# Float32 adjacency products as three one-pass products of split operands: a four-layer graph network on one core

## The chip, the core and the metric

The kernel runs on one core of a Trainium2 chip. The metric is the device time of one execution in microseconds (us). "Clock" is the mean granted TensorE clock of a stretch, as a share of full speed. Two kernels are compared by runs that alternate on the same chip.

## The reference

2708 nodes with 512 float32 features pass four layers, each followed by a residual and a layer norm. `adj` is a sparse float32 matrix, held densely.

```python
# layer 0: hypergraph mean
head = mask / maximum(sqrt(sum(mask * mask, -1)), EPS)      # mask = adj > 0
inc  = adj + head
x = LN(x + (inc @ x) / sum(inc, -1))
# layer 1: attention over adj's pattern, and a GCN, each with a gate
ga, gb = sigmoid([adj @ x, x] @ Wa.T + ba), sigmoid([adj @ x, x] @ Wb.T + bb)
h = x @ W_sa;  s = (h @ a_left)[:, None] + (h @ a_right)[None, :]
e = where(adj != 0, exp(-leaky_relu(s, 0.01)), 0)
attn = e / (sum(e, 1) + 1e-5)
x = LN(x + sigmoid(ga * (attn @ h) + gb * (adj @ (x @ W_gcn) + b_gcn)))
# layer 2: x W0 + A(x W1 + A(x W2 + A(x W3))), written as three hops
# layer 3: ((A x + x) / deg + x) @ W + b, relu
```

There are seven sweeps over a 2708 x 2708 matrix: one in layer 0, two in layer 1, three hops, one in layer 3. With 22 row tiles of 128 rows (the last has 20), a sweep is 22 x 22 = 484 products of a 128x128 block with 128x512 features.

## The kernel before

The sweeps' operands are float32 (only the 0/1 masks that are counted are 2-byte). The transposed adjacency block is the stationary operand and the features, resident in SBUF, are the moving one:

```python
def sweep_mm(ps, lhs, rhs, m, q, first=True, last=True):
    ...
    for k in range(k0, k1):
        kr = rows[k]
        nc.tensor.matmul(ps[:w], lhs[q][:kr, k - k0, :w], rhs[k][:kr], start=first and k == 0,
                         stop=last and k == NT - 1)
```

Row sums (layer 0's degree and the attention's denominator) are mostly VectorE work. Each piece of 5 or 6 blocks is reduced to one block, and TensorE only finishes the sum over partitions, four small products per row tile:

```python
def part_sum(t, q, w):
    ...
    nc.vector.tensor_reduce(s[:, :w], t[:, :nk, :w].rearrange("p k i -> p i k"), AX.X, ALU.add)
    return s

def row_sum(parts, w, eps):
    ps = psum.tile([P, 1], F32, name="ps_s", bufs=2)
    for n, s in enumerate(parts):
        nc.tensor.matmul(ps[:w], s[:, :w], ones, start=n == 0, stop=n == len(parts) - 1)
    ...
```

Row m's masks, counts and edges are made while row m-1 or m-2 is multiplied. Layer 1 reads each adjacency row once and runs its two sweeps interleaved. A hop is nothing but `sweep_mm`, four transposes, four dense products and an eviction per row tile.

## Time and profile before

Median 3713.67 us, 3711.66 to 3713.99. The stages, from windows of the profile:

| stage | us | TensorE busy | VectorE busy |
|---|---|---|---|
| layer 0 | 592 | 97% | 64% |
| layer 1, both sweeps | 970 | 100% | 45% |
| x2 W3 | 90 | 96% | 20% |
| hops and layer 3 | 2058 | about 100% | 3% to 26% |

The lines behind it stand in the prediction. How to read them: a share near 100% with a chain of waits that is 99% TensorE means that, as things stand, nothing but less TensorE work can shorten the run.

### The profile page before, as it was taken

How to read it: one execution, taken by the hardware profiler on the slowest of the kernel's cores; microseconds unless marked ns; L12 is line 12 of the kernel's file. 1: busy time of each engine (PE TensorE's matmuls, PEld its weight loads, DVE VectorE, ACT ScalarE, POOL GpSimd, SP SyncE). 2: the span in 40 equal slices, each digit the busy share in tenths (PEclk: the TensorE clock that was granted, in tenths of full speed). 3: DMA queues.
4: the chain of work that ended last, by engine and by line, in shares of the span. 5: the costliest groups of instructions: out<-in, count | busy, mean ns of one | idle time of the engine just before them, and what ended most of it. 6: DMA issues, size and time to landing. Idle time of an engine off the chain costs nothing.

```text
span 3710.3 us, 25433 instructions
## 1 busy us (share of the span) xinstructions
PE 3679.8 (99%) x10340; PEld 1626.9 (44%) x10340; DVE 1057.5 (29%) x1807; ACT 265.2 (7%) x392; POOL 88.8 (2%) x249
## 2 busy tenths in 40 slices
PE   7999999999999999999999999999999999999999
PEld 3444444444444444344444434444344444344443
DVE  6676654444444444110000000000000001222222
ACT  0000001111111111110000000000000000000000
POOL 0000000000000000000000000000000000000000
PEclk9999999999999999999999999999999999999999
DMA  4222211111111110102222122222222221222220
GB/s 149 53 56 56 54 44 55 31 34 30 33 30 30 30 33 19 37 24 60 60 60 60 48 71 60 60 60 60 59 60 60 60 60 48 77 69 71 68 71 21
DMA packets 377865, 197.16 MB, mean 53 GB/s; under 512 B 27156, under 2 KB 368364, under 8 KB 377748
## 3 DMA queue, kind: packets, MB, share of 16 engines
q1 hardware_dynamic: 370278, 181.58, 18.8%
q10 hardware_dynamic: 7470, 13.95, 1.1%
q8 instruction: 82, 1.34, 0.1%
q14 instruction: 35, 0.29, 0.0%
HBM read 189.94 MB, written 5.55 MB: 53 GB/s over the span
## 4 chain that ended last, share of the span: by engine, by line
PE 99%; DMA 1%; DVE 0%; issue 0%; POOLq 0%; SPq 0%
PE acc L102 68%; PE ps_u L102 11%; PE acc L116 9%; PE ps_d L116 6%; PE ps_t L109 2%; PE ps_s L129 1%; PE ps_s L171 1%; PE ps_s L284 1%; PE ps_s L210 0%; DMA adj<-in_adjT 0%; DMA w<-in_w_hop 0%; PE ps_t L262 0%; PE ps_u L186 0%; DMA A<-in_x 0%; DVE tmp L192 0%; DVE y L380 0%
## 5 line engine op out<-in xcount | busy, mean ns | idle before, releaser
L102 PE MATMUL acc<-C,adj 128*128 128x512 f32 (+2 forms) x1936 | 855.4, 595 | 0.0
L102 PE MATMUL acc<-B,adj 128*128 128x512 f32 (+2 forms) x1936 | 853.5, 594 | 0.0
L102 PEld LDWEIGHTS acc<-B,adj 128*128 128x128 f32 (+2 forms) x1936 | 352.5, 186 | 462.3 <-issue 461.1
L102 PEld LDWEIGHTS acc<-C,adj 128*128 128x128 f32 (+2 forms) x1936 | 352.2, 186 | 462.7 <-issue 462.1
L102 PE MATMUL acc<-A,adj 128*128 128x512 f32 (+1 forms) x968 | 436.1, 600 | 2.3 <-DVE adj L194 2.3
L102 PE MATMUL acc<-C,edge 128*128 128x512 f32 (+1 forms) x968 | 436.0, 597 | 0.0
L102 PE MATMUL ps_u<-B,adj 128*128 128x512 f32 (+1 forms) x968 | 434.6, 595 | 0.0
L116 PE MATMUL acc<-w,xT 128*128 128x512 f32 (+1 forms) x704 | 324.7, 604 | 1.4 <-DMA w<-in_w_hop 1.4
L102 PEld LDWEIGHTS acc<-C,edge 128*128 128x128 f32 (+1 forms) x968 | 176.0, 185 | 248.0 <-issue 248.0
L111 ACT COPY xT<-ps_t 128x512 f32<-128x512 f32 (+1 forms) x154 | 87.7, 570 | 2748.9 <-PE ps_t L109 2741.6
L102 PEld LDWEIGHTS ps_u<-B,adj 128*128 128x128 f32 (+1 forms) x968 | 176.6, 186 | 229.3 <-issue 229.2
L102 PEld LDWEIGHTS acc<-A,adj 128*128 128x128 f32 (+1 forms) x968 | 174.2, 187 | 214.1 <-issue 195.6
L116 PE MATMUL ps_d<-w,xT 128*128 128x512 f32 (+1 forms) x528 | 243.5, 604 | 0.5 <-DVE y L380 0.5
L116 PEld LDWEIGHTS acc<-w,xT 128*128 128x128 f32 (+1 forms) x704 | 124.4, 186 | 182.6 <-issue 180.9
L358 DVE COPY C<-acc 128x512 f32<-128x512 f32 (+1 forms) x22 | 15.2, 692 | 494.2 <-PE acc L116 494.2
L358 DVE COPY B<-acc 128x512 f32<-128x512 f32 (+1 forms) x22 | 15.2, 691 | 494.2 <-PE acc L116 494.2
L116 PEld LDWEIGHTS ps_d<-w,xT 128*128 128x128 f32 (+1 forms) x528 | 92.8, 186 | 129.9 <-issue 128.4
L361 DVE TENSOR_TENSOR y<-acc,A 128x512 f32<-128x512 f32 (+1 forms) x22 | 15.2, 692 | 413.6 <-PE acc L116 413.4
L131 DVE TENSOR_SCALAR rd<-ps_s 128x1 f32<-128x1 f32 (+1 forms) x44 | 6.9, 157 | 431.2 <-PE ps_s L129 431.2
L122 DVE TENSOR_REDUCE part<-edge 128x128 f32<-128x768 f32 (+3 forms) x88 | 111.6, 1305 | 0.0
L122 DVE TENSOR_REDUCE part<-adj 128x128 f32<-128x768 f32 (+3 forms) x88 | 111.6, 1309 | 0.0
L372 DVE TENSOR_SCALAR edge<-adj 128x768 bf16<-128x768 f32 (+3 forms) x88 | 44.2, 509 | 208.4 <-PE ps_s L171 152.1
(72 smaller groups left out, 1477.5 us busy)
## 6 DMA issues: line engine op xcount, KB each, us to landing
adj<-in_adjT SPq DMA_DIRECT2D x252, 384.0 KB
adj<-in_adjT SPq DMA_DIRECT2D x126, 320.0 KB
adj<-in_adjT SPq DMA_DIRECT2D x126, 256.0 KB
A<-in_x ACTq DMA_DIRECT2D x21, 256.0 KB
out<-xa SPq DMA_DIRECT2D x21, 256.0 KB
w<-in_w_hop ACTq DMA_DIRECT2D x4, 1024.0 KB
adj<-in_adjT SPq DMA_DIRECT2D x126, 10.0 KB
w<-in_w_sa ACTq DMA_DIRECT2D x1, 1024.0 KB
```

Source lines behind the costliest of these rows:

```text
L102: nc.tensor.matmul(ps[:w], lhs[q][:kr, k - k0, :w], rhs[k][:kr], start=first and k == 0, stop=last and k == NT - 1)
L109: nc.tensor.transpose(ps[:, c, :w], src[:w, c * P : (c + 1) * P], ident[:w, :w])
L111: nc.scalar.copy(t[:, :, :w], ps[:, :, :w])
L116: nc.tensor.matmul(ps[:w], xT[:, c, :w], wt[:, c, :], start=first and c == 0, stop=c == DC - 1)
L122: nc.vector.tensor_reduce(s[:, :w], t[:, :nk, :w].rearrange("p k i -> p i k"), AX.X, ALU.add)
L129: nc.tensor.matmul(ps[:w], s[:, :w], ones, start=n == 0, stop=n == len(parts) - 1)
L131: nc.vector.tensor_scalar(rd[:w], ps[:w], eps, None, ALU.add)
L171: nc.tensor.matmul(ps[:w], mask[m][q][:, k - k0, :w], ones_bf, start=k == 0, stop=k == NT - 1)
L284: nc.tensor.matmul(pz[:w], xT[m][:, c, :w], wab_sb[:, c, :], start=c == 0, stop=c == DC - 1)
L358: nc.vector.tensor_copy(dst[m][:w], ps[:w])
L361: nc.vector.tensor_tensor(y[:w], ps[:w], x2[m][:w], ALU.add)
L372: nc.vector.tensor_scalar(t[:, : k1 - k0, :w], adj[m][q][:, : k1 - k0, :w], 0.0, None, ALU.not_equal)
```

## The change

A float32 product takes, as the prediction reads its 0.86 us, four passes of 0.215 us through the array. The intent is to take three: split each operand into a rounded high part and a remainder, take hi·H and lo·L into one PSUM bank and a mixed product mx·G into another, and recombine the two banks at eviction. The operands are float32r, a 4-byte type whose product takes one pass. Features are split once per sweep, adjacency blocks anew in every sweep, on VectorE.

```diff
+    def split(a, nk, h=None):
+
+        s = slot(F32, "s")
+        lo = slot(F32R, "lo")
+        mx = slot(F32R, "mx")
+        av = a[:, :nk, :].bitcast(F32)
+        nc.vector.tensor_scalar(s[:, :nk, :].bitcast(I32), a[:, :nk, :].bitcast(I32), HI, None, ALU.bitwise_and)
+        nc.vector.tensor_tensor(lo[:, :nk, :], av, s[:, :nk, :], ALU.subtract)
+        nc.vector.scalar_tensor_tensor(mx[:, :nk, :], s[:, :nk, :], C1, av, ALU.mult, ALU.subtract)
... (hi: a copy of s by ScalarE in layer 0, by DMA in attention, else the block itself)
     def sweep_mm(...)
-            nc.tensor.matmul(ps[:w], lhs[q][:kr, k - k0, :w], rhs[k][:kr], start=first and k == 0,
-                             stop=last and k == NT - 1)
...
+            nc.tensor.matmul(pq, hi[:kr, b, :], H[k][:kr], start=first, stop=False)
+            nc.tensor.matmul(pq, lo[:kr, b, :], L[k][:kr], start=False, stop=last)
+            nc.tensor.matmul(pv, mx[:kr, b, :], G[k][:kr], start=first, stop=last)
+            if rs is not None:
+                nc.tensor.matmul(rs, hi[:kr, b, :], ones_r[:kr], start=first, stop=False)
+                nc.tensor.matmul(rs, lo[:kr, b, :], ones_r[:kr], start=False, stop=last)
...
+    def evacuate(acc, w):
+
+        pq, pv = acc
+        t = row_tile("t")
+        nc.scalar.mul(t[:w], pv[:w], -SC)
+        y = row_tile("y")
+        nc.vector.scalar_tensor_tensor(y[:w], pq[:w], C1, t[:w], ALU.mult, ALU.add)
+        return y
...
+    def run(load, prepare, before=None, finish=None, wide=True, rowsum=False, moving=None, early=None, ahead=2):
...
+            loads(n + ahead + 3)
+            prep(n + ahead)
+            if q == 0:
+                acc[m] = accumulators(wide and m == 2)
+                rs[m] = bank("rs", [P, 2]) if rowsum else None
+            sweep_mm(acc[m], ops.pop((m, q)), q, rs[m])
...
+            step()
+            if q == NQ - 1:
+                steps += finish(m, acc.pop(m), rs.pop(m))
```

`prep` issues the splits two pieces ahead of the products, and `step` one part of the previous row's end. With it come, cut here: row sums by two-column TensorE products (`ones_r` is [P, 2]) in place of VectorE's reductions; three resident feature tensors H, L, G, so that the features themselves pass through DRAM; a blocked adjacency copy in DRAM, stored in layer 0 and read by the later sweeps; a ring of 16 slots shared by adjacency, splits and edges; layer 0's masks on ScalarE from a second load of the adjacency; two exponentials per block on ScalarE; attention aggregates x1 and multiplies by W_sa afterwards; plain sweeps start with three row tiles side by side.

## The prediction

> **What bounds the kernel now.** I read the busy shares first, then the 40 slices, the chain that ended last, the costliest groups, then windows cut at the seven stages and the timeline inside one sweep.
>
> The page's busy shares, two of its slice rows and the head of its chain:
>
> ```profile
> PE 3679.8 (99%) x10340; PEld 1626.9 (44%) x10340; DVE 1057.5 (29%) x1807; ACT 265.2 (7%) x392; POOL 88.8 (2%) x249
> ...
> PE   7999999999999999999999999999999999999999
> ...
> DVE  6676654444444444110000000000000001222222
> ...
> PE 99%; DMA 1%; DVE 0%; issue 0%; POOLq 0%; SPq 0%
> PE acc L102 68%; PE ps_u L102 11%; PE acc L116 9%; PE ps_d L116 6%; PE ps_t L109 2%; PE ps_s L129 1%; PE ps_s L171 1%; PE ps_s L284 1%; PE ps_s L210 0%; DMA adj<-in_adjT 0%; DMA w<-in_w_hop 0%; PE ps_t L262 0%; PE ps_u L186 0%; DMA A<-in_x 0%; DVE tmp L192 0%; DVE y L380 0%
> ```
>
> TensorE is full in every slice but the first. 79% of the chain is L102, the adjacency sweeps; 15% is L116, the dense products. VectorE is idle in the hops. So only less TensorE work can help, and VectorE has room to pay for it. The stages, as windows (layer 0, layer 1, x2 W3, three hops, layer 3; columns: length, then busy time of each engine, clock, DMA share, GB/s):
>
> ```profile
> 0.00:592.30 592.30, 572.74 (x2099) 272.63 (x2100) 379.82 (x643) 26.13 (x44) 29.65 (x75) 1.00 0.25 67
> 592.30:1562.00 969.70, 969.07 (x2580) 431.55 (x2578) 437.57 (x675) 176.46 (x238) 17.12 (x43) 1.00 0.12 32
> 1562.00:1652.10 90.10, 86.72 (x257) 41.09 (x258) 18.02 (x28) 12.46 (x22) 0.54 (x1) 0.98 0.03 12
> 1652.10:2161.50 509.40, 509.40 (x1234) 217.21 (x1233) 15.22 (x23) 12.54 (x22) 4.42 (x22) 1.00 0.23 60
> ...
> 3180.30:3710.30 530.00, 523.02 (x1716) 230.24 (x1714) 140.09 (x307) 12.54 (x22) 16.65 (x43) 1.00 0.23 63
> ```
>
> A hop is 100% TensorE. Inside it, the timeline shows the unit of work:
>
> ```profile
> 1666.12 0.19 PEld L102 LDWEIGHTS acc<-B,adj 128*128 128x128 f32 x1 [0.24 <-issue]
> 1666.55 0.19 PEld L102 LDWEIGHTS acc<-B,adj 128*128 128x128 f32 x1 [0.24 <-issue]
> 1666.98 0.19 PEld L102 LDWEIGHTS acc<-B,adj 128*128 128x128 f32 x1 [0.24 <-issue]
> ```
>
> One weight load and one 512-column matmul record every 0.43 us, the load hidden. A float32 product is two such records (484 products give x968 for a sweep in the page's groups), so 0.86 us. A row tile of a hop, 22 products, four transposes, four dense products, takes 509.4/22 = 23.15 us.
>
> **What the Trainium skill says.** "FP8 and Floating Point Precision", section TensorE Precision Notes: float32 takes four passes, while reduced-precision float32 reads the 4-byte value truncated to FP22. The trace fits four passes: 0.86 us is four times 0.215. "TensorE: Matmul & The Clock Gate", section Back-to-back issue gap: warm, N/2.4 + 2.5 ns, which is 216 ns at 512 columns; the trace agrees (0.43/2), at a granted clock of 0.999. (That section also gives 131 ns as a sustained figure; nothing here is near it.) "VectorE: DVE Perf Modes", the perf-mode tier table: float32 tensor_scalar in SBUF runs at twice the rate, tensor_tensor at the single rate. The trace agrees: over 768 elements 540 ns against 952.
>
> **The change, part by part.**
>
> (1) Sweep products. hi*H + lo*L into one bank, mx*G into another, recombined at eviction, gives the full product in three one-pass matmuls. 7 sweeps x 484 = 3388 products: removed 3388 x 0.862 = 2920 us; added 10164 x 0.217 (0.215 plus a little) = 2206 us. Gain 715 us, if a one-pass load hides too. The load row lasts 190 ns, but eight loads of the row sums' one-column products come in 0.97 us, so 0.12 us each is the rate; below 0.217, so I assume hidden. Per row tile 66 x 0.217 = 14.3 us against 19.0.
>
> (2) Row sums move to TensorE in layers 0 and 1: 2 x 484 x 2 = 1936 two-column products, each with its own weight load. Cost by that 0.12 us: 232 us, 5.3 us per row tile. They replace VectorE reductions (223 us) and 336 small records (40 us).
>
> (3) Dense products stay 616 float32 ones (layer 0 loses its W_sa product, the attention sweep gains it behind the aggregation): 3.54 us per row. Transposes go from 616 to 704: 0.44 us per four.
>
> (4) VectorE splits every adjacency block anew in every sweep: a bitwise tensor_scalar, a subtraction, a scalar_tensor_tensor. Durations from the 640 and 768 rows, scaled linearly: two-tensor operations 817 and 951 give 684 ns at 512 elements and 550 at 384; tensor_scalar 485 and 540 give 430 and 375. A piece of four blocks is 430 + 2 x 684 = 1.80 us, of three 1.48; a row tile, four and two of these, 10.1 us. Layer 0 and attention have two more two-tensor operations per piece: + 7.7. The hop with the degree mask: + 2.5. Each feature tile entering a sweep is split for 1.8 us, 39.5 us per sweep, six times. VectorE in all: 1562 + 339 + 54 + 237 + evictions 106 + norms 138 + some 190 = about 2630 us, 77% of the new time: busy, but beside TensorE.
>
> (5) DMA: layer 0 loads the adjacency twice and stores the blocked copy; attention adds 32 MB of SBUF-to-SBUF copies (484 blocks of 64 KB); features go through DRAM. Before, the windows moved 60 GB/s at a share of 0.23, so twice to three times that has room; in a plain sweep 1.4 MB per 18.3 us is 79 GB/s.
>
> By stage (us per row tile, then the stage):
> - Layer 0: TensorE 14.3 + 5.3 + 0.55 (counts) + 0.44 + 0.3 + 0.8 = 21.7; VectorE 10.1 + 7.7 + 4.0 = 21.8. Both full: 22 x 21.8 + 39.5 (features) + 22 (first matmul, as before) = 541 as a floor. The sync queue carries some 22 transfers per row, the stores waiting for loads that just started. With 10% for coupling, 590. Before: 592.
> - Layer 1, plain sweep: 14.3 + 3.54 + 0.44 + 0.8 = 19.1, so 420, and 25 for the start (below): 445. Attention: 14.3 + 5.3 + 3.54 + 0.6 = 23.7 against VectorE 22.0 and ScalarE some 16 (44 exponentials of 128 columns, about 0.31 us by the slope of 843 and 737); 521 + 25 for coupling = 546. Sum 991. Before: 970. No gain.
> - x2 W3: 95 (before 90).
> - Hops: 14.3 + 3.54 + 0.44 = 18.3, so 403, each; the one with the mask 424, the others 430 with the start. Before 509 each.
> - Layer 3: 430 + 12 tail = 442. Before: 530.
>
> The start of a plain sweep: three row tiles run side by side while features are split: VectorE 3 x 10.1 + 39.5 = 70 us against TensorE's 3 x 14.3 = 43; 27 us exposed, some of it beside the end of the last sweep; I take 25.
>
> Sum: 590 + 991 + 95 + 424 + 430 + 430 + 442 = 3402; the bare TensorE sum is 22 x (21.7 + 19.1 + 23.7 + 4.1 + 18.8 + 3 x 18.3) = 3130. I add 30 for waits that I can't place: **3430 us, 8% faster.** Nearly all of the gain is in hops and layer 3.
>
> **The rivals.**
> (a) *One-pass matmuls are not 0.217 us.* If weight load and matmul no longer overlap fully, each costs up to 0.12 more: at 0.25 the time is 3770, slower. For the overlap: loads hidden at 44% busy before. Against: this trace has no one-pass 512-column matmul, and the load would be at 88% of its 190 ns. The float32 transposes, one pass, 128 columns, take 274 ns against 217 at 20 columns: 0.53 ns per column, near one column per cycle. That speaks for full rate.
> (b) *VectorE becomes the bound.* In layer 0 and attention it stands within 2 us of TensorE per row; if bitwise gets no double rate, + 1.4 us per row: VectorE 23.2, some 40 us in the two stages and 6 in each start, 3500.
> (c) *The sync queue or the shared 16-slot ring holds layer 0 and attention* (a piece takes up to six slots): 28 us per row in both would be + 100, 3530.
> (d) *Everything hides* and coupling is small: 3280.
>
> **Range and chances.** (b) and (c) together give the upper end 3620, (d) nearly the lower, 3310. Only (a), or queue trouble in every sweep, passes 3640, where the gain falls under 2%: same 0.09, slower 0.05, faster 0.86.
>
> **What the new profile would show.** (1): weight loads every 0.215 to 0.22 us inside a hop, 18.3 us per row tile, 403 to 430 us per hop. (2): row sums at about 0.12 us. (4): rows of 430 and 684 ns; VectorE near 75%, over 85% in layer 0. Layers 0 and 1 about as long as before. TensorE gaps of some 25 us at the start of plain sweeps, ended by VectorE. Wrong if: the spacing is over 0.24 us (a), or layers 0 and 1 together exceed 1700 us, the queue's loads waiting on TensorE or on stores (c).

## The result

The changed kernel is correct and takes 3941.8 us, median of 4 runs (3937.36 to 3948.46). The ratio to the kernel before is 1.062, 95% interval 1.060 to 1.063: **6.2% slower**.

The page after: busy shares, three slice rows, and the engines of the chain that ended last.

```profile
PE 3658.9 (93%) x15400; PEld 2664.6 (68%) x15400; DVE 2455.6 (62%) x4887; ACT 951.9 (24%) x2114; POOL 96.7 (2%) x172
...
PE   6999989899998888888889999999999999989999
...
DVE  7665656765553555555554666676555866687776
...
PEclk9888888899997887788789999999999999999999
...
PE 71%; issue 12%; DVE 8%; DMA 4%; ACT 4%; POOL 1%; SPq 0%; DVEq 0%; POOLq 0%; ACTq 0%
```

Two things are new. The chain is only 71% TensorE. And the clock row, solid before, shows 7s and 8s in slices 2 to 8 and 13 to 21. TensorE "busy" hardly fell, 3680 to 3659 us, because an instruction at half clock is busy for longer. In the attention sweep the step from a lo·L product to the next product is 0.234 us at full clock and 0.427 us at half (medians), so the matmuls bear the clock record out.

Windows at the stages (layer 0; plain sweep of layer 1; attention sweep; x2 W3; hops and layer 3; columns: length, busy time of TensorE, its weight loads, VectorE, ScalarE and GpSimd, then clock, DMA share, GB/s):

```profile
0.00:750.60 750.60, 655.57 (x3188) 524.43 (x3189) 480.51 (x1019) 255.77 (x485) 49.24 (x106) 0.84 0.52 150
750.60:1214.00 463.40, 451.56 (x1891) 329.92 (x1889) 269.53 (x521) 72.81 (x131) 0.00 (x0) 0.99 0.31 92
1214.00:2049.40 835.40, 707.54 (x2724) 526.16 (x2723) 463.34 (x899) 391.14 (x1103) 11.82 (x22) 0.79 0.31 101
2049.40:2157.70 108.30, 106.68 (x334) 52.37 (x334) 44.43 (x78) 48.47 (x85) 0.25 (x1) 0.99 0.20 58
2157.70:3937.00 1779.30, 1737.54 (x7279) 1231.74 (x7277) 1197.76 (x2370) 183.72 (x311) 35.36 (x44) 1.00 0.35 107
```

| stage | before | predicted | after |
|---|---|---|---|
| layer 0 | 592 | 590 | 751 |
| layer 1 | 970 | 445 + 546 = 991 | 463 + 835 = 1299 |
| x2 W3 | 90 | 95 | 108 |
| hops, layer 3 | 2058 | 1726 | 1779 |

The gain came where it was predicted, 279 us in the last four sweeps. It was more than eaten by layer 0 (+159) and layer 1 (+329), the two places where sweeps carry row sums, at clocks of 0.84 and 0.79. Every stage without row sums ran at 0.99 or 1.00.

What waits there? The waits of the attention sweep (engine, instruction, what released it: us in total, times, longest):

```profile
DVE e L451 <- ACT s L450: 152.9, 25, 8.4
DVE rd L462 <- PE rs L184: 123.8, 21, 7.1
...
PE accv L181 <- DVE mx L160: 103.6, 64, 8.5
```

and of layer 0, from 120 us to its end:

```profile
DVE r L312 <- PE cnt L301: 93.5, 18, 7.1
DVE rd L349 <- PE rs L184: 79.3, 20, 5.0
```

The 8.5 us before `mx` are the start of the sweep; the runs below that list this wait whole show them too. `rd` is the reciprocal of the row sum, the first thing that VectorE does for a finished row, and it needs the row's last row-sum product. The timeline at one row end of the attention sweep shows what that does (start, us, engine, line, instruction, and the idle time before it with its releaser):

```profile
1632.30 0.16 DVE L462 TENSOR_SCALAR rd<-rs 128x1 f32<-128x1 f32 x1 [7.13 <-PE rs L184]
1632.37 0.68 DVE L198 SCALAR_TENSOR_TENSOR y<-accq,t 128x512 f32<-128x512 f32 x1
...
1632.97 0.42 DVE L158 TENSOR_SCALAR s<-e 128x512 int32<-128x512 int32 x1
...
1634.03 0.68 DVE L160 SCALAR_TENSOR_TENSOR mx<-s,e 128x512 fp32r<-128x512 f32 x1
...
1634.77 0.80 PE L181 MATMUL accv<-G,mx 128*128 128x512 f32 x1 [2.51 <-DVE mx L160]
```

VectorE stood still for 7.13 us because `rd` came ahead of the next row's splits in its queue. When the row sum came, the splits started, and TensorE in turn waited 2.51 us for them. The same stretch, cut into windows of 4 us (the clock is the third number from the end):

```profile
1616.00:1620.00 4.00, 3.61 (x20) 2.85 (x18) 3.02 (x8) 2.48 (x9) 0.55 (x1) 1.00 0.42 132
1620.00:1624.00 4.00, 2.50 (x8) 1.82 (x9) 3.79 (x9) 2.37 (x8) 0.00 (x0) 0.79 0.42 138
1624.00:1628.00 4.00, 4.00 (x11) 2.70 (x11) 1.13 (x2) 0.00 (x0) 0.00 (x0) 0.50 0.75 244
1628.00:1632.00 4.00, 4.00 (x13) 3.22 (x12) 0.00 (x0) 2.93 (x9) 0.00 (x0) 0.50 0.00 0
```

After an interrupted stretch (2.50 of 4 us busy) the clock drops to 0.50, and **stays there although TensorE is then busy 4.00 of 4.00 us, twice**. So there are two suspects: VectorE's queue order, and a clock that does not come back. A third was a rival, the shared ring and the queue of loads. For the loads the waits themselves speak: in the whole attention sweep TensorE's matmuls waited 2.9 us for DMAs, its weight loads 19.9. In layer 0, ScalarE's masks waited 61.6 us for the second load of the adjacency; e6 comes back to that.

In a hop nothing of this happens. TensorE's matmuls follow one another like this:

```profile
2399.87 0.39 PE L179 MATMUL accq<-H,a 128*128 128x512 f32 x1
...
2400.10 0.39 PE L180 MATMUL accq<-L,lo 128*128 128x512 f32 x1
...
2400.32 0.39 PE L181 MATMUL accv<-G,mx 128*128 128x512 f32 x1
```

The mean of 1180 such spacings in two stretches of the last sweeps is 0.228 us, against 0.217 predicted.

### The clock record

The trace also lists each change of the granted clock. Added up for the attention sweep and for layer 0 (its first 40 us left out), for the kernel after and for the experiments below:

| kernel | attention: us, stretches at half clock (mean us) | layer 0: us, stretches at half clock (mean us) |
|---|---|---|
| before | whole layer 1: 970, none | 592, none |
| after | 835, 27 (13.0) | 751, 25 (10.1) |
| e1 attention queue order | 770, 24 (13.1) | 751, 27 (9.0) |
| e2 no row sums | 665, 27 (4.3) | 693, 22 (9.9) |
| e4 no count in layer 0 | 832, 27 (13.3) | 577, 13 (5.5) |
| e5 256-column row sums | 739, 22 (3.9) | 604, 7 (7.8) |
| e10 64-column row sums | 832, 26 (13.7) | 624, 13 (7.4) |
| e6 both layers reordered | 753, 23 (11.1) | 632, 10 (5.1) |
| e9 reordered, 256 columns | 627, 4 (6.8) | 617, 3 (6.8) |
| e11 reordered, no row sums | 625, 21 (7.5) | 614, 19 (4.0) |
| e12 after's order, 256 columns | 762, 32 (3.8) | 730, 21 (9.6) |
| e13 e5's order, 2 columns | 819, 27 (11.9) | 655, 21 (7.5) |
| e14 e6's order, 256 columns | 718, 23 (6.8) | 624, 4 (7.7) |

Every one of these stretches is a whole multiple of 3.41 us long. In "after" the attention's are mostly five of them (13 of 27), 17.1 us.

### The profile page after: what moved, and what is told of

Same layout as the page of the kernel before. It is cut to its first block, busy times and chain, and to the rows that moved or that the text cites. A ratio compares the mean times of both kernels' runs of the same rounds, so it can differ in the third digit from the quotient of the medians.

```text
span 3937.0 us, 44473 instructions
## 1 busy us (share of the span) xinstructions
PE 3658.9 (93%) x15400; PEld 2664.6 (68%) x15400; DVE 2455.6 (62%) x4887; ACT 951.9 (24%) x2114; POOL 96.7 (2%) x172
## 4 chain that ended last, share of the span: by engine, by line
PE 71%; issue 12%; DVE 8%; DMA 4%; ACT 4%; POOL 1%; SPq 0%; DVEq 0%; POOLq 0%; ACTq 0%
PE accq L179 19%; PE accq L180 17%; PE accv L181 16%; PE ps_d L218 14%; DMA a<-in_adjT 2%; PE ps_t L210 2%; PE rs L184 1%; DVE mx L160 1%; ACT mask L292 1%; DVE s L158 1%; DMA hi<-s 1%; ACT mask L293 1%; POOL rstd L228 1%; DVE cv L111 1%; DVE e L452 1%
## 5 line engine op out<-in xcount | busy, mean ns | idle before, releaser
L181 PE MATMUL accv<-G,mx 128*128 128x512 f32 (+1 forms) x3388 | 1341.1, 420 | 126.6 <-DVE mx L160 123.4
L180 PE MATMUL accq<-L,lo 128*128 128x512 f32 (+1 forms) x3388 | 1375.9, 414 | 10.6 <-ACT L L112 10.5
L179 PE MATMUL accq<-H,a 128*128 128x512 f32 x2420 | 1023.7, 427 | 19.5 <-ACT H L109 19.2
L181 PEld LDWEIGHTS accv<-G,mx 128*128 128x128 f32 (+1 forms) x3388 | 656.6, 198 | 316.8 <-DVE mx L160 145.2
L180 PEld LDWEIGHTS accq<-L,lo 128*128 128x128 f32 (+1 forms) x3388 | 682.2, 202 | 139.7 <-issue 30.0
L159 DVE TENSOR_TENSOR lo<-a,s 128x512 fp32r<-128x512 f32 (+1 forms) x660 | 426.3, 646 | 447.4 <-PE accq L179 437.0
L218 PE MATMUL ps_d<-w,xT 128*128 128x512 f32 (+1 forms) x1232 | 585.5, 612 | 24.6 <-ACT xT L212 18.6
L179 PEld LDWEIGHTS accq<-H,a 128*128 128x128 f32 x2420 | 452.0, 188 | 202.3 <-issue 71.4
L179 PE MATMUL accq<-H,hi 128*128 128x512 f32 x968 | 556.1, 574 | 31.0 <-ACT hi L163 26.1
L160 DVE SCALAR_TENSOR_TENSOR mx<-s,a 128x512 fp32r<-128x512 f32 (+1 forms) x660 | 421.5, 639 | 0.4 <-PE accq L179 0.4
L451 DVE TENSOR_TENSOR e<-e,s 128x512 f32<-128x512 f32 x132 | 84.6, 641 | 152.9 <-ACT s L450 152.9
```

The source lines that it names most:

```text
L159: nc.vector.tensor_tensor(lo[:, :nk, :], av, s[:, :nk, :], ALU.subtract)
L160: nc.vector.scalar_tensor_tensor(mx[:, :nk, :], s[:, :nk, :], C1, av, ALU.mult, ALU.subtract)
L179: nc.tensor.matmul(pq, hi[:kr, b, :], H[k][:kr], start=first, stop=False)
L180: nc.tensor.matmul(pq, lo[:kr, b, :], L[k][:kr], start=False, stop=last)
L181: nc.tensor.matmul(pv, mx[:kr, b, :], G[k][:kr], start=first, stop=last)
L218: nc.tensor.matmul(ps[:w], xT[:, c, :w], wt[:, c, :], start=c == 0, stop=c == DC - 1)
```

## The experiments

Fourteen kernels ran. All edit the changed kernel, unless said otherwise. The expectations are those before each ran; where they say "the changed kernel's" they compare with 3941.8 us. Runs without an interval are one time each, of unknown state, beside the kernel before on the same chip (3712 to 3714 us in all of them). Kernels of this family that ran more than once spread over 4 to 12 us, and stage lengths come from one profiled run, so differences of some 10 us mean nothing here. The compiler orders each engine's instructions by its own estimate of their times, so an edit may also move instructions that it doesn't touch; e12 to e14 were made because that had happened. The traces show it in e2, e3 and e4 as well: against the changed kernel at least 115, 559 and 210 of VectorE's instructions stand in other places.

### e1: the row end behind the next row's splits, in attention

Theory: queue order on VectorE costs the stage its time. Rival: the row-sum products with their low array work do. Edit, with an instruction-order hint that places the row end's VectorE and ScalarE work behind the splits already issued:

```diff
+            marks = last_on(nc.vector, nc.scalar)
             prep(n + ahead)
 ...
-                steps.pop(0)()
+                f, first = steps.pop(0)
+                if first and marks and (rowsum and early is None):
+                    behind(marks, f)
```

> Attention sweep only: the row sum's reading and the eviction of a finished row are queued on VectorE and ScalarE behind the splits (and exponentials) of the next row's first two pieces; same instructions, correct result. Order theory (VectorE waits about 7 us per row for the end of the row with the next row's splits behind it, TensorE then starves and its clock is halved): the attention sweep falls from 820 us to 580 to 650 with a granted clock over 0.93, the kernel to 3700 to 3780. Row-sum theory (the two-column products keep the array too idle for the full clock): the sweep stays within 40 us of 820 and the clock under 0.85.

Measured: 3872.61 us, correct; attention 770 us instead of 835. Neither theory's range. TensorE's waits for `mx` fell from 103.6 us (64 times) to 57.4 (44 times), each with the 8.5 us of the start, so order was a cost; but the clock of the stage stayed at 0.80. Windows of 2 us of this kernel show why:

```profile
1614.00:1616.00 2.00, 0.17 (x3) 0.09 (x1) 1.93 (x5) 1.41 (x5) 0.00 (x0) 1.00 0.35 131
...
1618.00:1620.00 2.00, 2.00 (x7) 1.71 (x8) 1.88 (x4) 0.25 (x1) 0.00 (x0) 0.50 0.55 152
...
1628.00:1630.00 2.00, 2.00 (x7) 1.70 (x6) 1.82 (x4) 0.00 (x0) 0.00 (x0) 0.50 0.97 304
1630.00:1632.00 2.00, 2.00 (x9) 1.69 (x8) 0.81 (x2) 0.00 (x0) 0.00 (x0) 0.67 0.26 97
```

One gap of 1.88 us, then some 13 us at half clock with TensorE busy 2.00 of 2.00 us in every window. The mean half-clock stretch did not shorten (13.1 us).

### e2: no row-sum products

A constant stands in for the sums. The result is wrong (relative error 0.177).

```diff
-            if rs is not None:
-                nc.tensor.matmul(rs, hi[:kr, b, :], ones_r[:kr], start=first, stop=False)
-                nc.tensor.matmul(rs, lo[:kr, b, :], ones_r[:kr], start=False, stop=last)
 ...
-                rs[m] = bank("rs", [P, 2]) if rowsum else None
+                rs[m] = fake_rs if rowsum else None
```

> Wrong result on purpose: the 1936 row-sum products of layer 0 and attention are left out, a constant takes their place. Row-sum theory: clock over 0.95 in both stages, layer 0 near 570 us and attention near 560, the kernel near 3500. Order theory: the products' own time goes (some 5 us per row, 110 us per stage), but the eviction still stands in front of the next row's splits, so idle TensorE and clock under 0.9 stay; layer 0 near 640, attention near 690, the kernel near 3700.

Measured: 3708.18 us. Attention went from 835 to 665, layer 0 from 751 to 693. The products' own time at full clock is 484 x 2 x 0.115 = 111 us a stage, and attention lost 170: more than they cost. The total is what the order theory had written (3700), the stages fit neither theory throughout. The clock record shows a change beside it. There are as many half-clock stretches as before (27), but they last 4.3 us and not 13.0. This suggested that the gaps start a stretch and that the row sums among the products keep it from ending. Layer 0 does not fit so plainly: its stretches stayed at 9.9 us, and it lost only 58 us. There the one-column count products and the waits between them were still in place.

### e3: a ring of 36 slots

The memory for it comes from putting G on L's tiles (wrong, relative error 0.237).

```diff
-    G = [feat.tile([P, D], F32R, name=f"G{t}", tag=f"G{t}") for t in range(NT)]
+    G = L
-    RING = 16
+    RING = 36
```

> Wrong result on purpose: the third split of the features shares the second's buffers, which frees room for 36 ring slots in place of 16; instructions unchanged. Ring theory (six or seven slots per piece leave no lookahead): layer 0 and attention lose most of their waits, the kernel under 3650. Order theory: VectorE's order at the end of a row is the same as before, so attention stays within 40 us of 820 and the kernel above 3850.

Measured: 3920.64 us; layer 0 743, attention 824. More than twice the slots gave 21 us, and the waits of attention hardly changed (`rd` 123.5 us for 123.8, `mx` 100.6 for 103.6). That speaks against the prediction's rival (c), a ring that holds these two stages. It is not the ring alone that changed, though: 3500 of TensorE's 15400 matmuls stand in other places too.

### e4: layer 0 without the count

No second load, no masks on ScalarE, no one-column count products; a constant scale instead. The comparison with the reference still passed, but it computes another scale.

```diff
-        for q in range(NQ):
-            mask_piece(m, q)
-            count(ps, mask0.pop((m, q)), m, q)
-        ...
-        scale[m] = r
+        scale[m] = fake_r
```

> Wrong result on purpose: layer 0's count of positive entries (second load of the adjacency, two ScalarE mask operations per piece, 484 one-column products, the wait of VectorE for the count) is left out, a constant scales the mask. If that chain is what starves TensorE and halves its clock in layer 0: layer 0 falls from 752 us to under 620 with a clock over 0.93. If it is the eviction at the end of a row, as in attention, or the row sums: layer 0 stays above 680 with a clock under 0.88.

Measured: 3764.87 us. Layer 0 fell from 751 to 577, and its clock rose from 0.84 to 0.92. So most of layer 0's loss hangs on the count chain: the count of a whole row is issued at once, TensorE waits for ScalarE's masks piece by piece, and VectorE waits for the count (93.5 us, above).

### e5: row sums with 256 columns of ones

The row-sum products do more work in the array, in the same number of instructions. The result stays correct, as only column 0 is read.

```diff
-    ones_r = const.tile([P, 2], F32R, name="ones_r")
+    ones_r = const.tile([P, 256], F32R, name="ones_r")
-                rs[m] = bank("rs", [P, 2]) if rowsum else None
+                rs[m] = bank("rs", [P, 256]) if rowsum else None
```

> Correct result: each row-sum product has 256 columns of ones in place of 2, [...]the weight load (0.115 us each, measured) stays the limit; nothing else changes. If the clock stays halved for long after each gap because the row-sum products keep the array too idle: clock over 0.93 in both stages, attention under 720 us (835 before), layer 0 under 680 (751), the kernel under 3750, although TensorE does more. If only gaps set the clock: within 30 us of the changed kernel's time in each stage, clock within 0.03.

Measured: 3694.99 us, **247 us less for more work**; correct. Layer 0 604 at clock 0.96, attention 739 at 0.94. The wider products cost nothing where the clock is full. Weight loads in the changed kernel's attention sweep (two columns), then in this kernel's:

```profile
1617.04 0.19 PEld L183 LDWEIGHTS rs<-ones_r,hi 128*128 128x128 f32 x1
...
1617.27 0.19 PEld L184 LDWEIGHTS rs<-ones_r,lo 128*128 128x128 f32 x1
...
1617.38 0.19 PEld L179 LDWEIGHTS accq<-H,hi 128*128 128x128 f32 x1
```

```profile
1277.26 0.19 PEld L183 LDWEIGHTS rs<-ones_r,hi 128*128 128x128 f32 x1
...
1277.50 0.19 PEld L184 LDWEIGHTS rs<-ones_r,lo 128*128 128x128 f32 x1
...
1277.62 0.19 PEld L179 LDWEIGHTS accq<-H,hi 128*128 128x128 f32 x1
```

The steps are 0.23 and 0.11 us in one, 0.24 and 0.12 in the other: a product of 2 columns takes about as long as one of 256.

It looked as if this run separated the clock from everything else. It does not. A comparison of the two built programs showed that the compiler, reckoning with longer products, had also put 208 of VectorE's 4880 instructions in other places (and, by the traces, 227 of TensorE's). In layer 0 the row end's `rd` and eviction now stood two operations of the next piece further back, and the count's result one; in attention `rd` stood two further back, behind the eviction and one operation of the split. That is a small dose of e1's edit. The gain of 247 us is taken apart in e12 and e13. Of the expectation, attention's "under 720" was missed by 19 us.

### e6: both layers reordered, the count spread over the row

e1's order in both layers, with TensorE's row-end products queued behind as well; layer 0's masks and counts two pieces at a time.

```diff
-        if m + 1 < NT and q == 0:
-            scale0(m + 1)
-        if m + 1 < NT and q == 2:
-            scale_row(m + 1)
+            if q == 0:
+                ...
+                behind(last_on(nc.tensor), lambda: count0(m + 1, (0, 1)))
+                begin0(m + 1, (2, 3))
+            elif q == 1:
+                behind(last_on(nc.tensor), lambda: count0(m + 1, (2, 3)))
+                begin0(m + 1, (4, 5))
+            ...
```

> Correct result, same operations: in layer 0 and attention each finished row's work is queued behind the splits of the next row's pieces on VectorE, ScalarE and TensorE, and layer 0's mask operations and count products are spread over the row and queued behind sweep products. Chain theory (each engine waits in order behind a late result, TensorE runs dry, its clock is halved): layer 0 falls from 751 to 550 to 620 us and attention from 835 to 580 to 680, clock over 0.92 in both, the kernel 3470 to 3620. If the row sums alone hold the clock down: clock stays under 0.85, the kernel above 3750.

Measured: 3745.32 us (ratio to before 1.009, interval 1.007 to 1.011), correct. Layer 0 went to 632, with 10 half-clock stretches instead of 25; attention only to 753, its clock 0.83. Both miss the ranges written, layer 0 by 12 us and attention by 73, and the total lies just under the rival's 3750. Order repairs most of layer 0 and only part of attention. In layer 0 (first line, 79.3 us before) VectorE's wait for the row sum is all but gone. In attention it is gone from the list, but VectorE's wait for ScalarE's exponentials grew from 152.9 to 217.6 us (second line):

```profile
DVE rd L396 <- PE rs L184: 4.1, 1, 4.1
DVE e L498 <- ACT s L497: 217.6, 44, 10.8
```

ScalarE's masks still wait 65.9 us for their loads in this layer 0 (61.6 in the changed kernel). So those loads are not what had made it long.

### e10: row sums with 64 columns

e5's edit with 64 in place of 256.

> The changed kernel with 64 columns of ones instead of 2 (256 gave 3695). Activity theory, gradual: the array streams 64 of 512 columns more per row-sum product, some of the half-clock stretches shorten, time 3800 to 3900, clock of layer 0 and attention about 0.85 to 0.9. If activity counts against a threshold, it may fall at either end (3695 or 3942). Rival, that 256 columns helped for another reason than array work (only that the products take longer, so VectorE keeps ahead): 64 columns do not lengthen a weight-load-bound product, so nothing changes, 3942 within 15. Correct result.

Measured: 3808.3 us, clock 0.934; correct. Between this kernel and e5 the built order is the same on TensorE, VectorE, ScalarE and the sync engine, so these two differ in array work alone. In attention the 192 further columns are worth 93 us (832 to 739), and the stretches shrink from 13.7 to 3.9 us. In layer 0 they are worth 20 (624 to 604). In attention the effect is not gradual: 64 columns do nothing (e13, the same order with 2 columns, has 819), so the amount that counts lies between 64 and 256 there. In layer 0 it may be: 655 (e13), 624, 604.

### e9: both repairs together

e6 and e5's 256 columns in one kernel.

> Both repairs at once: row-end work and the layer 0 mask/count pieces queued behind (as in the run that reordered both layers), and row sums with 256 columns of ones. Apart they gave -196 us and -247 us against the changed kernel (3941.8). If order and clock are two causes that each cost their own time, the gains nearly add: about 3500 us, layer 0 near 560, attention near 650. My estimate lies between, 3570 (layer 0 580, attention 650), because a wait cured by order also spares the half clock that follows it. Rival, one cause only (the reordering helped only because fewer gaps halve the clock): the total stays within 40 us of the wide run alone, 3650 to 3700, with attention above 710. Correct result.

Measured: **3594.46 us**, ratio to before 0.968, interval 0.967 to 0.970; correct. Its windows of layer 0 and of attention:

```profile
0.00:616.90 616.90, 551.13 (x3189) 435.05 (x3190) 479.36 (x1022) 264.49 (x485) 41.50 (x106) 0.98 0.63 183
...
1080.10:1707.50 627.40, 581.43 (x2724) 437.85 (x2723) 464.58 (x900) 391.58 (x1103) 12.04 (x22) 0.98 0.41 134
```

Attention, 835 us after the change, is down to 627 with four half-clock stretches left, and the kernel beats the one before by 3%. The rival's range, 3650 to 3700 with attention above 710, is left behind. But the caution of e5 holds: against e6 the compiler had again moved things, 40 of VectorE's instructions, and on TensorE it spread the mx·G products of one piece in each row between other products instead of issuing them in a block (285 of TensorE's moved in all). e14 takes that apart.

### e12, e13 and e14: the order held fast

In these three, every engine is held to the order of another build, by tracing the program twice and chaining the second build's instructions in the first one's order. The traces confirm it: TensorE, VectorE and ScalarE ran in the same order as in the kernel compared with. e12 is the changed kernel's order with 256 columns, e13 is e5's order with 2 columns, e14 is e6's order with 256.

```diff
+    order = program(2, None)[2]              # e12; e13: 256 and then 2
+    nc, arrays, _ = program(256, order)
 ...
+                for name in order:
+                    i = traced[name]
+                    if i.engine in last:
+                        tc.add_manual_dep(i, last[i.engine], info, reason="order of the other program")
+                    last[i.engine] = name
```

> The changed kernel with 256 columns of ones, every engine held to exactly the changed kernel's order of instructions (the earlier run with 256 columns also had about 200 of VectorE's 4880 instructions in other places, since the compiler orders by its own estimates). If array work alone brings the clock back: layer 0 600 to 650, attention 740 to 790, half-clock stretches about 4 us in attention, total 3690 to 3780. If it was the other order: half-clock stretches stay near 13 us, layer 0 near 750, attention near 835, total above 3900. In between would mean both. Correct result.

> The counterpart: 2 columns of ones, every engine held to the order that the compiler gave the 256-column kernel. If array work is the cause, it is slow: attention 820 to 840 (as the run with 64 columns, which had this order too, 832), half-clock stretches near 13 us there; layer 0 then tells what the order is worth in it: 700 to 751 if array work cured it, 604 to 640 if the order did. If the order was the cause in both stages: total near 3695. Correct result.

> The kernel reordered in both layers (3745) with 256 columns of ones and exactly its own order of instructions, as the run of both repairs (3594) had some 40 VectorE instructions moved by the compiler as well. If array work is what that run gained: attention 620 to 670, total 3590 to 3640. If the compiler's moves did: attention stays above 720, total above 3700. Correct result.

Measured: e12 3842.98 us (4 runs, ratio to before 1.034, interval 1.033 to 1.036), e13 3826.08, e14 3696.64; all correct. With the runs above this is a table in which each row has one order, built identically but for the columns:

| order | layer 0, 2 columns | layer 0, 256 | attention, 2 columns | attention, 256 | total, 2 columns | total, 256 |
|---|---|---|---|---|---|---|
| the changed kernel's | 751 | 730 (e12) | 835 | 762 (e12) | 3942 | 3843 |
| the compiler's for 256 columns | 655 (e13) | 604 (e5) | 819 (e13) | 739 (e5) | 3826 | 3695 |
| e6's | 632 (e6) | 624 (e14) | 753 (e6) | 718 (e14) | 3745 | 3697 |
| the compiler's for e6 with 256 | not run | 617 (e9) | not run | 627 (e9) | not run | 3594 |

Both causes are real. Along a row, more array work and nothing else gives 99, 131 and 49 us; in attention 73, 80 and 35. The mean half-clock stretch there falls from 13.0 to 3.8 us (first row), from 11.9 to 3.9, and from 11.1 to 6.8. Down a column, order and nothing else gives 116 and then another 81 us at 2 columns, and 249 us at 256 (3843 to 3594); there e6's order is worth no more than the compiler's (3697 and 3695). In layer 0 order is most of it: 751 to 632 at 2 columns, where array work gave 21. Against the expectations: e12's attention (762) and its stretches came as written, its layer 0 did not (730, not 600 to 650), and so its total is 63 us over the range; most of layer 0's cure in e5 was the changed order (96 us) and not the columns (51). e13's layer 0 of 655 lies between its two cases. e14's attention missed its range by 48 us and all but met the rival's (above 720); the compiler's further moves are worth 91 there (718 to 627). With them VectorE's wait for the exponentials fell from 181.5 to 103.6 us and TensorE's for `mx` from 75.8 to 33.2.

That the wider products are only slower, and so let VectorE keep ahead (the rival in e10's expectation), does not fit. The four steps hi·H, lo·L and two row sums of a block take 0.688 us at full clock and 1.281 at half in the changed kernel's attention, 0.697 and 1.280 in e12's (sums of medians from the traces). And the number of half-clock stretches did not fall, 27 to 32; only their length did.

Two waits of e12's attention sweep, to set beside those of the changed kernel:

```profile
PE accv L181 <- DVE mx L160: 97.5, 49, 8.5
DVE rd L462 <- PE rs L184: 76.4, 21, 4.7
```

The order is the same and so is the count of 21, but VectorE's wait for the row sum is 76.4 us instead of 123.8 and the longest 4.7 instead of 7.1. A stretch at half clock delays the row sum, on which VectorE waits, which delays the splits, on which TensorE waits: clock and order make each other worse.

### e11: reordered, no row sums

e6 with e2's edit; wrong (relative error 0.177).

> The reordered kernel with the row-sum products removed and a constant in their place; wrong result on purpose. Removing them alone left attention at 665 us at clock 0.91 and layer 0 at 693. If in-order queues explain the rest of the attention's excess over one-pass time (three products x 0.231 x 484 = 335 us plus row-end work 50), it falls to 560 to 600 and layer 0 to 550 to 590, total about 3500. Rival, the chain of exps on ScalarE and six VectorE passes per piece is itself the bound there (VectorE busy 460 us plus waits for ScalarE): attention stays at 640 to 665.

Measured: 3592.95 us; layer 0 614, attention 625 at clock 0.87. Attention lies between the two ranges. Layer 0 is 24 us over what was written. The kernel is no faster than e9, which does the row sums as well. Its 21 stretches at half clock last 7.5 us: here too the clock was lost, without any two-column product. Keeping the row sums with 256 columns, in e9's order, was as good as leaving them out. TensorE's waits for `mx` were 79.1 us in that sweep (48 times), so part of the chain through ScalarE and VectorE is a bound of its own; it was not taken apart further.

### e8: 2-byte operands in the sweeps

All sweep operands in bfloat16, the high part replaced by the remainder (wrong, relative error 1.41). It asks what the spacing of 0.228 us is made of (the expectation has 0.231 for it).

```diff
-F32R = mybir.dt.float32r
+F32R = mybir.dt.bfloat16
```

> Wrong result on purpose: all sweep operands are bfloat16 (the first product uses the second's weights), so weight loads move half the bytes; the number and shape of matmuls stays. If the 4-byte weight load is what stretches a one-pass product from 0.216 to 0.231 us: spacing 0.215 to 0.219 us inside a hop, a hop falls from 440 to about 420 us. If not: spacing within 0.003 of 0.231.

Measured: 3617.29 us. The spacing in two stretches of the last sweeps is 0.2159 us (1159 spacings), against 0.2279. The predicted 0.217 is thus what 2-byte operands take, and 4-byte ones take 0.012 us more. Weight loads last 0.10 us instead of 0.19. The run does not separate the stationary from the moving operand, both being 4 bytes wide in one kernel and 2 in the other.

### e7: three passes only where nothing else is needed

Layers 0 and 1 from the kernel before, layers 2 and 3 from the kernel after; the blocked copy is stored in layer 1. The edit in outline:

```diff
 # the kernel before, from layer 2 on
+    # ---- layers 2 and 3, on split operands ----
+    ph.close()                       # frees layer 0's and 1's buffers
...
+    run(load_blk, prepare3, before3, hop_finish(2, Y0), wide=False, early=early2)
...
```

> Correct result: layers 0 and 1 as in the kernel before (float32 products, reductions on VectorE), with the blocked copy stored in layer 1; layers 2 and 3 as in the changed kernel. If the change pays where TensorE is fed and loses only in layers 0 and 1: 592 + 970 for the first two, 1887 for the rest as measured in the changed kernel, about 3450 us, 7% under before, clock over 0.98. If the split sweeps owe their time to something that layers 0 and 1 leave behind, over 3550.

Measured: **3471.64 us**, 4 runs, ratio to before 0.935, interval 0.934 to 0.937; correct, clock 0.994. It beats both kernels.

## Why the prediction was wrong

It said 3430 us and 8% faster; the chip said 3942 and 6.2% slower. The miss is 512 us. By stage: layer 0 +161, the plain sweep of layer 1 +18, attention +289, x2 W3 +13, hops and layer 3 +53, less the 30 that was set aside, 504; another 5 us is the time outside the span, and the rest is rounding. (A slip of no weight: layer 0's 541 with 10% is 595, not 590.)

**The step that failed** is the stage sum for layer 0 and attention: "TensorE 14.3 + 5.3 + ... = 21.7; VectorE ... 21.8. Both full", with "10% for coupling" and 25 us of it for attention. It took each engine's busy time and let the larger set the stage. Two assumptions were hidden in it, and both fell:

- *Two full engines overlap.* VectorE kept to the order of its queue (it stood still for 7.13 us at `rd`, with the next splits behind it), and this order put a wait for TensorE's last row-sum product (in layer 0 also for the count) ahead of the work that TensorE needed next. 10% did not cover that. Order alone gave 201 us of the 450 by which the two stages exceed the prediction (751 + 835 to e6's 632 + 753), and at 256 columns 248 us (e12's 730 + 762 to e9's 617 + 627). By these edits it is the larger cause, above all in layer 0, where array work alone gave 21, 51 and 8 us in the three orders.
- *The clock stays at 1.00.* The prediction read "a granted clock of 0.999" from a kernel whose TensorE hardly paused (969.07 of 969.70 us busy in layer 1), and carried it to stages in which it pauses at every row end. The clock measured 0.84 and 0.79. In the changed kernel's own order, array work alone gave back 21 + 73 = 94 us (e12). The Trainium skill, "TensorE: Matmul & The Clock Gate", section What's actually happening, describes a gate with a half and a full rate and windows of about 3.4 us; the prediction cited that page for its issue gap only. The trace agrees with the two rates and with the window (stretches of whole multiples of 3.41 us). It does not agree that about one busy window brings the full rate back: e1 shows some 13 us without a pause at 0.50. What the row sums add to TensorE's load is little in *time* (step 2's 0.12 us measured 0.115, right), but they dilute the array's work.

What is left in e9 over the prediction is 27 us in layer 0 and 81 in attention. The first lies within the coarseness of such a sum. For attention a sum from measured durations would be, as an estimate, 1452 x 0.228 + 968 x 0.115 + 88 x 0.88 + some 16 = 536 us of TensorE, and TensorE's busy time there was 581. The difference and the 46 us of pauses were not pursued; the largest wait left on VectorE is that for the exponentials, 103.6 us.

**A mis-sized term:** "10164 x 0.217" measured 0.228, so 112 us. In the five plain sweeps, 7260 products x 0.011 = 80 us, which covers their miss (18 + 53 = 71) fully. The prediction took 0.217 from float32 passes, where a 4-byte weight serves two passes of one record; e8 shows that 2-byte operands reach it and 4-byte ones do not.

**What was right:** where the gain lies (279 us in hops and layer 3, 332 predicted); the row sums' time; VectorE's durations, its total being 2456 us against 2630; the start of plain sweeps. **The rivals:** (a) is the size of 0.011 us, not of 0.12. (b) is not the bound: VectorE is 62% busy. (c), ring and queue of loads, was named for the right stages with the wrong cause: e3 speaks against the ring, and e6 repairs most of layer 0 while the waits for its loads stay. The "wrong if" clause gave the symptom, layers 0 and 1 over 1700 us (2050 measured), and the wrong reason, loads waiting on TensorE. None of the four named the clock.

What stays open: how much array work, over what time, the clock asks for. 64 columns did not suffice in attention and 256 did; the kernels here do not resolve it further. That array work is the quantity is shown as far as e12 against the changed kernel, and e10 against e5, differ in nothing else; no counter of it was read. What remained in attention beyond the two causes, and why the compiler's last moves are worth 91 us, is open as well.

## What to carry to other kernels

When two engines are both near full, the larger sum of busy times is a floor and not an estimate: write down the order of each in-order queue at a row end, and see which wait stands ahead of work that the other engine needs; and compare the order of two built programs before you put a difference down to the edit alone. Before moving small reductions to TensorE "because it costs only 0.12 us", see whether the engine pauses nearby; if the clock row shows 5s to 8s while TensorE is busy, widen the small products' moving operand first, as it may cost no time at all. And apply a change like this where the profile shows the other engines idle: here layers 2 and 3 alone gave 6.5%, while the whole conversion lost 6.2%.

## What the Trainium skill lacked or had wrong

- "TensorE: Matmul & The Clock Gate", Part 1, says that about 3.4 us of sustained work restores the full clock. Here matmuls mixed with two-column products kept TensorE without a pause for some 13 us at 0.50 after a gap of 1.88 us (e1); with 256 columns in the same products and the same order the mean half-clock stretch fell from 13.0 to 3.8 us (e12). The page lacks that a mix of light products can hold the clock at half.
- The same page, section Why this matters for your kernels, warns of gaps over about 3 us. A gap of 1.88 us was enough here (e1), and of the 24 half-clock stretches of that sweep 23 had no gap over 2.5 us in or reaching into the 3.41 us before them.
- The same page, section Back-to-back issue gap: its 216 ns at 512 columns held for bfloat16 operands (0.2159 us, e8) and not for float32r ones (0.2279 us). No page was found to say that 4-byte one-pass operands space wider.
